# Banks, product buffers and the order of sums in a message-passing layer on one core

## The chip, the core and the metric

The kernel runs on one core of one Trainium2 chip, as one launch. The time is the device time in microseconds (us) of an execution. The kernel before was timed in three runs. A profile was taken of a further execution.

## What is computed

One layer of a graph network over 6,250 nodes of 128 features and 100,000 edges, which are sorted by their destination `dst`, all in float32:

```
msg_in = concatenate([x[src], x[dst], edge_attr], axis=1)      # 128 + 128 + 4
h = silu(msg_in @ mW1 + mb1)
messages = h @ mW2 + mb2
aggregated = segment_sum(messages, dst, N)
u = silu(concatenate([x, aggregated], axis=1) @ uW1 + ub1)
updated = u @ uW2 + ub2
out = layernorm(x + layer_norm(x + updated, ln_g, ln_b))
```

## The kernel before, in words

Edges are handled in 98 groups of 1,024 (G = 8 tiles of 128; the last group has 6 tiles). The first product is split: `x @ mW1[:128]` and `x @ mW1[128:256] + mb1` are computed once per node and kept as two tables in HBM, `tab_a` and `tab_b` (the table phase, L333 to L362). For an edge, `pre` is a row of `tab_a` (by its source), a row of `tab_b` (by its destination) and the four edge attributes times their weights. Since edges are sorted, the destinations of a group lie within a window of W = 96 nodes. So no second gather is needed: 96 rows of `tab_b` and the 4 rows of weights are loaded as the matrix `mv`, and a matrix `st` holds, for each edge, a one at its destination and its attributes. TensorE multiplies the two.

For each group g these steps are made; the names are those of the code.

- `fetch` (L272): eight gathers on GpSimd's queue (POOL), each of 128 rows of `tab_a` into the tile `ga`. `ga` has six buffers (AHEAD + 2), and gathers are issued four groups ahead. Groups 0 to 3 (RAW = 4) gather rows of x itself, since the table isn't there yet; gathers from group 4 on wait for `tab_a` to be written.
- `load` (L532): SP loads `mv` and the attribute rows of `st`, four groups ahead.
- `node_matrix` (L541): VectorE makes `st` (L543), three groups ahead.
- `products` (L564): TensorE's matmuls of `st` and `mv` into `pre` (L568). `pre` is a PSUM tile of two banks with three buffers, and products are made two groups ahead of their use.
- `hidden` (L577): VectorE adds `ga` and `pre` to `s` (L590), ScalarE applies silu and writes `h` (L591). For groups 0 to 3 TensorE transposes the rows (L583) into another `pre` buffer, VectorE copies them (L585), TensorE multiplies them by the weights (L572, between the matmuls of L568), and ScalarE applies silu (L586).
- `edge_matrix` (L553): VectorE makes `oh` (L556), the edges' one-hot matrix of the window, by comparing the node row `w_row` (0 to 95) with each edge's place `rel`; one group ahead.
- `by_nodes` (L594): TensorE transposes the counts of edges (L597) and sums h by node with `oh` (L600).
- `add` (L603): VectorE adds the sums to `acc` and the counts to `deg` (L606), at the window's place.

A node batch (`node_batch`, L410) computes the rest of the layer for four tiles of nodes as soon as their sums are complete, a stage per group (`advance`), with its products in the PSUM tile `y` of one bank; the last batch follows the last group.

The order on SP, TensorE, VectorE and ScalarE is the order of the code (`manual_schedule`, L107). In the step of group g of the loop at L613, that is: fetch g+4, load g+4, products g+2, hidden g, node_matrix g+3, edge_matrix g+1, by_nodes g-1, add g-2, and a stage of each running node batch. So the sums of a group stand behind the products of three groups later, and one step behind their h. On GpSimd's queue, the order within a group's gathers is left to the scheduler.

[...] `pre` takes six, `y` one, and `held_ps` (L169) one: it holds the sums of even groups, the sums of odd groups, and the node row `w_row` (L170).

Further, `hold` (L260) adds waits for TensorE to gathers. In the table phase one gather each of groups 2 and 3 waits for matmuls of that phase (L358); in the loop, one gather of each group from 9 on waits for the products of four groups before (L287).

Of the kernel before, what the change touches and what calls it, by code (L numbers as in the profile page):

```python
# [24 lines left out]
def kernel(  # L25
# [81 lines left out]
    edges.enter_context(tc.manual_schedule(engines={ENG.SP, ENG.PE, ENG.DVE, ENG.Activation}))  # L107
    gath = edges.enter_context(tc.tile_pool(name="gath", bufs=AHEAD + 2))
    work = edges.enter_context(tc.tile_pool(name="edge", bufs=2))
    ps = edges.enter_context(tc.tile_pool(name="edge_ps", bufs=2, space=PSUM))  # L110

    def wide():
        return ps.tile([P, G, P], F32, name="pre", bufs=3)

    def narrow():
        return wide()[:, :2, :].rearrange("p i f -> p (i f)")

    tables = ExitStack()
    tpool = tables.enter_context(tc.tile_pool(name="tables", bufs=1, side="right"))


    def by_group(a, pad):
# [43 lines left out]
    make_identity(nc, ident)  # L166
    w_row_i = consts.tile([P, W], I32, name="w_row_i")
    nc.gpsimd.iota(w_row_i, pattern=[[1, W]], base=0, channel_multiplier=0)
    held_ps = fixed.tile([P, 5 * W], F32, name="held_ps")  # L169
    w_row = held_ps[:, 4 * W :]  # L170
    nc.vector.tensor_copy(w_row, w_row_i)
    p_col_i = consts.tile([P, 1], I32, name="p_col_i")
    nc.gpsimd.iota(p_col_i, pattern=[[0, 1]], base=0, channel_multiplier=1)
# [81 lines left out]
    tab_b = dram.tile([NW, H], F32, name="tab_b")  # L255
    ea_d = dram.tile([ED, NG * GE], F32, name="ea_d")
    near_d = dram.tile([NG, GE], U8, name="near_d")
    rows, bases, near, opening, made = {}, {}, {}, {}, {}

    def hold(g, ins):  # L260

        tc.add_manual_dep(
            opening[g],
            ins.ins.name,
            mybir.DependencyInfo(mybir.DependencyClass.Sync, mybir.DependencyReason.DATA),
            reason="TensorE keeps up with the gathers",
        )

    def tiles_of(g):
        return min(G, -(-(E - g * GE) // P))  # L270
# [1 line left out]
    def fetch(g):  # L272
        if g >= NG:
            return
        rows[g] = gath.tile([P, G, H], F32, name="ga")
        for i in range(tiles_of(g)):
            ins = nc.gpsimd.indirect_dma_start(  # L277
                out=rows[g][:, i, :],
                out_offset=None,
                in_=x if g < RAW else tab_a[:, :],  # L280
                in_offset=bass.IndirectOffsetOnAxis(
                    ap=src_i[:, g, i : i + 1] if g else src_0[:, i : i + 1], axis=0
                ),
            )
            if i == 0:
                opening[g] = ins.ins
                if g - AHEAD in made:  # L287
                    hold(g, made[g - AHEAD])

    for g in range(RAW):  # L290
        fetch(g)
# [47 lines left out]
    for k, (i0, n) in enumerate(parts):  # L339
        if k + 1 < len(parts):  # L340
            turn_x(*parts[k + 1])

        tb = x_sb[:, i0 : i0 + n, :]
        ta = tpool.tile([P, G, H], F32, name="t", bufs=2)
        for j0, m in groups(n, G // 2):
            pm = wide().rearrange("p (i s) f -> p i s f", s=2)
            for j in range(m):
                cols = slice((i0 + j0 + j) * P, (i0 + j0 + j + 1) * P)
                ins = nc.tensor.matmul(pm[:, j], xT[:, cols], w1, start=True, stop=True)  # L349
            own = slice(j0, j0 + m)  # L350
            nc.scalar.copy(ta[:, own], pm[:, :m, 0, :])
            nc.vector.tensor_add(  # L352
                tb[:, own], pm[:, :m, 1, :], b1[:, None, :].to_broadcast([P, m, H])
            )
        nc.sync.dma_start(by_node(tab_b)[:, i0 : i0 + n, :], tb)
        nc.sync.dma_start(by_node(tab_a)[:, i0 : i0 + n, :], ta[:, :n])
        if k in (1, 3):
            hold(k // 2 + 2, ins)  # L358
        cols = slice(i0 * P, NW if i0 + n == NT else (i0 + n) * P)
        nc.vector.memset(acc[:, cols], 0.0)  # L360
        nc.vector.memset(deg[:, cols], 0.0)
# [6 lines left out]
    if E < NG * GE:  # L368
        pad = tpool.tile([ED, NG * GE - E], F32, name="pad")
        nc.vector.memset(pad, 0.0)  # L370
        nc.sync.dma_start(ea_d[:, E:], pad)
    tables.close()


    w2u = consts.tile([P, H], F32, name="w2u")
# [20 lines left out]
            nc.sync.dma_start(t, row.rearrange("(o f) -> o f", o=1).to_broadcast([P, H]))  # L396

    def fuse_weights():
        pt = narrow()
        nc.tensor.transpose(pt[:, :P], raw_w["w2"], ident)  # L400
        w2T = work.tile([P, P], F32, name="w2T", bufs=1)
        nc.scalar.copy(w2T, pt[:, :P])
        pm = narrow()
        nc.tensor.matmul(pm[:, :H], w2T, raw_w["u1a"], start=True, stop=True)
        nc.tensor.matmul(pm[0:1, H:], raw_w["mb2"], raw_w["u1a"], start=True, stop=True)
        nc.scalar.copy(w2u, pm[:, :H])
        nc.scalar.copy(mb2u, pm[0:1, H:])


    def node_batch(i0, n, work, new, y):  # L410
# [83 lines left out]
        yield  # L494
        nc.sync.dma_start(rows_of(out), o[:m, :n])

    def node_tiles(pool, ps):
        return (
            pool,
            lambda name, p=P: pool.tile([p, BT, H], F32, name=name),  # L500
            lambda: ps.tile([P, BT, H], F32, name="y"),
        )

    def advance(running):

# [9 lines left out]
        hbuf.append(held.tile([P, G, H], F32, name=f"h{k}"))  # L515
    NST = 5
    nodes = edges.enter_context(tc.tile_pool(name="nodes", bufs=1))
    node_ps = edges.enter_context(tc.tile_pool(name="node_ps", bufs=1, space=PSUM))
    stbuf = [held.tile([K1, GE], F32, name=f"st{k}") for k in range(NST)]

    def load_bases(g):
# [40 lines left out]
        return oh  # L562

    def products(g, xg=None):  # L564
        pre = wide()
        st = stbuf[g % NST].rearrange("k (i c) -> k i c", i=G)
        for i in range(tiles_of(g)):
            ins = nc.tensor.matmul(  # L568
                pre[:, i, :], st[:, i, :], mv[g % NM], start=True, stop=xg is None
            )  # L570
            if xg is not None:
                nc.tensor.matmul(pre[:, i, :], xg[:, i, :], w1[:, 0, :], start=False, stop=True)  # L572
        if xg is None:
            made[g] = ins
        return pre

    def hidden(g):  # L577
        h = hbuf[g % NH]
        ga = rows.pop(g)
        if g < RAW:  # L580
            px = wide()
            for i in range(G):
                nc.tensor.transpose(px[:, i, :], ga[:, i, :], ident)  # L583
            xg = work.tile([P, G, P], F32, name="s")
            nc.vector.tensor_copy(xg, px)  # L585
            nc.scalar.activation(h, products(g, xg), AF.Silu)  # L586
        else:
            n = tiles_of(g)
            s = work.tile([P, G, H], F32, name="s")
            nc.vector.tensor_add(s[:, :n], ga[:, :n], pre.pop(g)[:, :n])  # L590
            nc.scalar.activation(h[:, :n], s[:, :n], AF.Silu)  # L591
        return h

    def by_nodes(g, h, oh):  # L594

        pt = held_ps[:, g % 2 * 2 * W : (g % 2 + 1) * 2 * W]
        nc.tensor.transpose(pt[0:1, W:], deg_g[:, g : g + 1], ident[:W, :W])  # L597
        n = tiles_of(g)
        for i in range(n):
            nc.tensor.matmul(pt[:, :W], h[:, i, :], oh[:, i, :], start=i == 0, stop=i == n - 1)  # L600
        return pt
# [11 lines left out]
    for g in range(NG + 1):  # L613
        if g == 3:
            load_weights()
        if g == 5:
            fuse_weights()
        for c in range(1, NC):
            if g == max(1, c * EC // GE - 10):
                attributes(c)  # L620
            if g == max(1, c * EC // GE - 10) + 1:
                attribute_rows(c)
        if g + AHEAD >= RAW:
            fetch(g + AHEAD)
        if g + LEAD < NG:
            load(g + LEAD)
        if g >= RAW:
            for k in range(g if g == RAW else g + MADE - 1, min(g + MADE, NG)):
                pre[k] = products(k)
        if g < NG - 1:  # L630
            h[g] = hidden(g)
        if g + MADE < NG:
            node_matrix(g + MADE)
        if g + 1 < NG:
            oh[g + 1] = edge_matrix(g + 1)
        if 0 <= g - 1 < NG:
            pt[g - 1] = by_nodes(g - 1, h.pop(g - 1), oh.pop(g - 1))
        for k in range(max(g - 2, 0), g - 1 if g < NG - 1 else g):
            if k in pt:
                add(k, pt.pop(k))  # L640
        for i0, n, first in batches:
            if g == min(first + 1, NG):
                tiles = node_tiles(nodes, node_ps)
                if first == NG:

                    tiles = (
                        nodes,
                        lambda name, p=P: gath.tile([P, G, H], F32, name="ga")[:p, :BT],
                        lambda: wide()[:, :BT],
                    )  # L650
                running.append(node_batch(i0, n, *tiles))
        advance(running)
        if g >= NG - 2:
            advance(running)
        if g == NG - 1:
            h[g] = hidden(g)
    while running:
        advance(running)
    edges.close()
# [1 line left out]
    def all_nodes():  # L661
        with tc.tile_pool(name="nodes_g", bufs=2) as nodes:
            with tc.tile_pool(name="nodes_g_ps", bufs=1, space=PSUM) as node_ps:
                for i0, n, _ in batches:
                    running = [node_batch(i0, n, *node_tiles(nodes, node_ps))]
                    while running:
                        advance(running)

# [145 lines left out]
```

## Time and profile before

| | |
|---|---|
| three timed runs | 1029.84, 1030.1 and 1032.72 us; median 1030.1 us |
| profiled execution | 1330.47 us, span 1328.6 us |
| mean granted clock of TensorE | 0.678 |
| POOL (gathers) | busy 738.9 us in 790 instructions, 782 of them gathers of 943 ns |
| TensorE's matmuls | busy 685.9 us |
| VectorE | busy 485.2 us |
| ScalarE | busy 238.9 us |
| DMA | 88.95 MB, 67 GB/s over the span |

The profiled execution is one execution, and longer than the timed runs by 300 us. "Span" is from the program's first instruction to its last. In rows of the timeline the first number is the start, the second the time taken, both in us; then engine, line, operation and the tiles written and read; in brackets stands the engine's idle time ahead of the row and what ended it. In rows of the waits: who waited, for whom, the sum in us, how many times, and the longest. "issue" means that the profile shows nothing that was waited for, "remote" a semaphore whose last update it can't put to an instruction.

### The profile page before, as it was taken

Reading aid. Unit: us, or ns where it says so; the run is one execution under the profiler, and the core shown is the slowest. Engines: PE = TensorE matmul, PEld = TensorE weight load, DVE = VectorE, ACT = ScalarE, POOL = GpSimd, SP = SyncE. Lnnn points to the kernel's source line nnn. Section 1 sums busy time; section 2 is a strip of 40 time slices with the busy share of each in tenths; the row PEclk is TensorE's granted clock in tenths of the full one; section 3 lists DMA queues with packets and bytes.
Section 4 is the critical chain, followed back from the end, with each engine's and each line's share of the span. In section 5 each row is a group of like instructions: output and inputs, shape, how many; then the busy total and the mean of one; then the engine's idle time right before and its main releaser. Section 6 shows DMA issues by size and latency. Waiting matters only on the chain.

```text
span 1328.6 us, 11337 instructions
## 1 busy us (share of the span) xinstructions
PE 685.9 (52%) x3696; PEld 605.2 (46%) x3696; DVE 485.2 (37%) x1018; ACT 238.9 (18%) x294; POOL 738.9 (56%) x790
## 2 busy tenths in 40 slices
PE   3737756434733553455563364445544555543665
PEld 3526645433633453355453354345433445443553
DVE  1643333243334333334233334233334334334443
ACT  1301111012112111112121112111202202202223
POOL 6266666645654655566655655555655666645500
PEclk9867777666766675676666767666866766766765
DMA  6733222112312212222212211222212222212100
GB/s 171 214 94 82 70 62 78 50 36 54 93 44 67 72 47 63 54 69 70 76 45 64 70 51 49 76 54 68 79 44 60 60 67 74 73 42 54 50 7 24
DMA packets 69916, 88.95 MB, mean 67 GB/s; under 512 B 20671, under 2 KB 51534, under 8 KB 69850
## 3 DMA queue, kind: packets, MB, share of 16 engines
q0 software_dynamic: 25024, 51.30, 15.3%
q1 hardware_dynamic: 41290, 35.08, 9.2%
q10 hardware_dynamic: 3536, 1.77, 0.5%
q8 instruction: 31, 0.51, 0.2%
q14 instruction: 35, 0.29, 0.1%
HBM read 76.71 MB, written 11.38 MB: 66 GB/s over the span
## 4 chain that ended last, share of the span: by engine, by line
another core or an unknown queue 34%; issue 23%; DVE 21%; PE 11%; POOL 6%; DMA 3%; DVEq 1%; ACT 1%; SPq 0%; ACTq 0%; POOLq 0%
DVE st L543 7%; PE held_ps L600 6%; POOL ga L277 6%; DVE oh L556 5%; DVE s L590 2%; PE pre L568 2%; DVE z L476 1%; DVE y L473 1%; DMA ga<-tab_a,src_i 1%; DVE st L427 1%; DVE mv L428 1%; DVEq L590 1%; PE y L446 1%; DMA mv<-tab_b 1%
## 5 line engine op out<-in xcount | busy, mean ns | idle before, releaser
L277 POOL DMA_INDIRECT ga<-tab_a,src_i x750 | 707.5, 943 | 495.5 <-issue 371.7
L597 PE MATMUL held_ps<-ident,deg_g 96*1 96x96 f32 x98 | 28.6, 292 | 533.5 <-DVE oh L556 474.1
L606 DVE TENSOR_TENSOR acc<-acc,held_ps 128x96 f32 x98 | 24.9, 254 | 730.7 <-remote 497.6
L600 PE MATMUL held_ps<-oh,h 128*128 128x96 f32 x1564 | 287.7, 362 | 0.3 <-ACT h L591 0.3
L600 PEld LDWEIGHTS held_ps<-oh,h 128*128 128x128 f32 x1564 | 276.9, 274 | 1.6 <-ACT h L591 0.7
L568 PE MATMUL pre<-mv,st 100*128 100x128 f32 x1564 | 260.6, 327 | 31.4 <-issue 31.4
L568 PEld LDWEIGHTS pre<-mv,st 100*128 100x128 f32 x1564 | 245.7, 242 | 41.5 <-issue 40.0
L597 PEld LDWEIGHTS held_ps<-ident,deg_g 96*1 96x1 f32 x98 | 8.2, 83 | 551.5 <-DVE oh L556 487.2
L591 ACT ACTIVATE h<-s 128x1024 f32<-128x1024 f32 x94 | 99.1, 1054 | 713.3 <-DVE s L590 576.8
L543 DVE TENSOR_SCALAR_CACHE_REDUCE st<-near,p_next 96x1024 f32<-96x1024 uint8 x98 | 124.2, 1269 | 1.6 <-DMA ea_d<-pad 1.6
L590 DVE TENSOR_TENSOR s<-ga,pre 128x1024 f32<-128x1024 f32 x94 | 114.4, 1217 | 28.1 <-DMA ga<-tab_a,src_i 10.7
L556 DVE TENSOR_TENSOR oh<-held_ps,rel 128x768 f32<-128x768 f32 x98 | 93.0, 949 | 0.0
L591 ACT ACT_TABLE_LOAD x21 | 26.9, 1283 | 124.3 <-DVE s L590 83.2
L349 PE MATMUL pre<-w,xT 128*128 128x256 f32 x98 | 25.9, 420 | 12.9 <-DVE x_sb L352 11.7
L277 POOL DMA_INDIRECT ga<-in_x_dram,src_i x24 | 22.6, 943 | 15.6 <-PE pre L349 6.9
L433 ACT ACT_TABLE_LOAD x24 | 30.8, 1283 | 2.7 <-DVE mv L428 2.3
L462 PEld LDWEIGHTS y<-u,uT 128*128 128x128 f32 x94 | 22.7, 327 | 17.6 <-issue 17.6
L572 PE MATMUL pre<-w,s 128*128 128x128 f32 x64 | 18.4, 383 | 21.0 <-DVE s L585 15.9
L349 PEld LDWEIGHTS pre<-w,xT 128*128 128x128 f32 x98 | 20.0, 211 | 17.3 <-DVE x_sb L352 13.2
L462 PE MATMUL y<-u,uT 128*128 128x128 f32 x94 | 26.2, 460 | 0.0
L441 ACT COPY acc_b<-acc 128x512 f32<-128x512 f32 (+1 forms) x12 | 7.3, 609 | 102.0 <-DVE acc L606 66.4
L572 PEld LDWEIGHTS pre<-w,s 128*128 128x128 f32 x64 | 15.0, 289 | 21.8 <-DVE s L585 16.3
(117 smaller groups left out, 399.4 us busy)
## 6 DMA issues: line engine op xcount, KB each, us to landing
ga<-tab_a,src_i POOLq DMA_INDIRECT x750
near<-near_d SPq DMA_DIRECT2D x24, 384.0 KB
mv<-tab_b SPq DMA_DIRECT2D x98, 48.0 KB
tab_b<-x_sb SPq DMA_DIRECT2D x6, 512.0 KB
tab_a<-t SPq DMA_DIRECT2D x6, 512.0 KB
xs<-in_x_dram SPq DMA_DIRECT2D x11, 256.0 KB
out_dram<-z SPq DMA_DIRECT2D x11, 256.0 KB
st<-ea_d SPq DMA_DIRECT2D x98, 16.0 KB
```

The lines of the kernel that those rows point to most:

```text
L277: ins = nc.gpsimd.indirect_dma_start(out=rows[g][:, i, :], out_offset=None, in_=x if g < RAW else tab_a[:, :], in_offset=bass.IndirectOffs ...
L349: ins = nc.tensor.matmul(pm[:, j], xT[:, cols], w1, start=True, stop=True)
L433: nc.scalar.activation(r[:, :n], mv[:, :n, 1], AF.Sqrt, bias=eps)
L462: nc.tensor.matmul(y[:, i, :], by_p[:, :, i], u2, start=False, stop=i == n - 1)
L543: nc.vector.tensor_scalar(stbuf[g % NST][:W], near.pop(g), p_next, 0.0, op0=OP.is_equal, op1=OP.add, accum_out=deg_g[:, g : g + 1],)
L556: nc.vector.tensor_tensor(oh, w_row[:, None, :].to_broadcast([P, G, W]), rel[:, g, :, None].to_broadcast([P, G, W]), op=OP.is_equal,)
L568: ins = nc.tensor.matmul(pre[:, i, :], st[:, i, :], mv[g % NM], start=True, stop=xg is None)
L572: nc.tensor.matmul(pre[:, i, :], xg[:, i, :], w1[:, 0, :], start=False, stop=True)
L590: nc.vector.tensor_add(s[:, :n], ga[:, :n], pre.pop(g)[:, :n])
L591: nc.scalar.activation(h[:, :n], s[:, :n], AF.Silu)
L597: nc.tensor.transpose(pt[0:1, W:], deg_g[:, g : g + 1], ident[:W, :W])
L600: nc.tensor.matmul(pt[:, :W], h[:, i, :], oh[:, i, :], start=i == 0, stop=i == n - 1)
```

## The change

- The node row `w_row` becomes a tile of its own, in a bank of its own.
- The sums go to `pt`, a tile of one bank with two buffers, so that even and odd groups have a bank each.
- `pre` has two buffers instead of three. The table phase has its own pool with three buffers of two banks, which is closed before the loop's PSUM tiles are made.
- In the step of group g, products of g+2 come after hidden g (the add of `ga` and `pre`, which frees a buffer), and the sums of g come right behind that in the same step, where before those of g-1 stood. The adds of g-2 stay, and stand ahead of the sums.
- The holds of gathers are taken out.
- `fuse_weights`, once, at group 5, uses the tile of the node batches instead of a `pre` buffer.

```diff
-    ps = edges.enter_context(tc.tile_pool(name="edge_ps", bufs=2, space=PSUM))
+    tables_ps = tables.enter_context(tc.tile_pool(name="tables_ps", bufs=3, space=PSUM))
     def wide():
-        return ps.tile([P, G, P], F32, name="pre", bufs=3)
+        return tables_ps.tile([P, G, P], F32, name="wide")
...
-    held_ps = fixed.tile([P, 5 * W], F32, name="held_ps")
-    w_row = held_ps[:, 4 * W :]
+    w_row = fixed.tile([P, W], F32, name="w_row")
...
-            if i == 0:
-                opening[g] = ins.ins
-                if g - AHEAD in made:
-                    hold(g, made[g - AHEAD])
...
-        if k in (1, 3):
-            hold(k // 2 + 2, ins)
...
     tables.close()
+    ps = edges.enter_context(tc.tile_pool(name="edge_ps", bufs=2, space=PSUM))
+    node_ps = edges.enter_context(tc.tile_pool(name="node_ps", bufs=1, space=PSUM))
+    def rows_ps():
+        return ps.tile([P, G, P], F32, name="pre")
+    def node_y():
+        return node_ps.tile([P, BT, H], F32, name="y")
...
     def by_nodes(g, h, oh):
-        pt = held_ps[:, g % 2 * 2 * W : (g % 2 + 1) * 2 * W]
+        pt = ps.tile([P, 2 * W], F32, name="pt")
...
-        if g >= RAW:
-            for k in range(g if g == RAW else g + MADE - 1, min(g + MADE, NG)):
+        if g == RAW:
+            for k in (g, g + 1):
                 pre[k] = products(k)
-        if g < NG - 1:
+        last = g >= NG - 1
+        if not last:
             h[g] = hidden(g)
+        if g >= RAW and g + 2 < NG:
+            pre[g + 2] = products(g + 2)
         if g + MADE < NG:
             node_matrix(g + MADE)
         if g + 1 < NG:
             oh[g + 1] = edge_matrix(g + 1)
-        if 0 <= g - 1 < NG:
-            pt[g - 1] = by_nodes(g - 1, h.pop(g - 1), oh.pop(g - 1))
-        for k in range(max(g - 2, 0), g - 1 if g < NG - 1 else g):
+        for k in range(g - 2, g - 1 if not last else g):
             if k in pt:
                 add(k, pt.pop(k))
+        if not last:
+            pt[g] = by_nodes(g, h.pop(g), oh.pop(g))
...
         if g == NG - 1:
-            h[g] = hidden(g)
+            pt[g] = by_nodes(g, hidden(g), oh.pop(g))
```

## The prediction

> **What bounds the kernel now.** I read the first part of the page for the engines' shares, the waits, and then the timeline, first of the gather queue alone and then of all engines.
>
> ```profile
> PE 685.9 (52%) x3696; PEld 605.2 (46%) x3696; DVE 485.2 (37%) x1018; ACT 238.9 (18%) x294; POOL 738.9 (56%) x790
> ```
> ```profile
> DVE acc L606 <- remote: 497.6, 42, 17.4
> PE held_ps L597 <- DVE oh L556: 474.1, 54, 18.1
> POOL ga L277 <- issue: 380.6, 734, 10.3
> ```
>
> No engine is full. The second and third lines are two halves of one loop. TensorE's sums (L597, L600) wait for the edge matrix (L556), and VectorE's adds (L606) wait for the sums: the node row, which L556 reads, and both halves of the sums lie in one bank, `held_ps`. But 1330.5 us is the profiled execution's time, against a median of 1030.1 us, so I ask which waits the timed runs can hold.
>
> ```profile
> 599.37 0.94 POOL L277 DMA_INDIRECT ga<-tab_a,src_i  x1 [0.30 <-issue]
> 600.62 0.94 POOL L277 DMA_INDIRECT ga<-tab_a,src_i  x1 [0.30 <-issue]
> ...
> 609.71 0.94 POOL L277 DMA_INDIRECT ga<-tab_a,src_i  x1 [3.16 <-issue]
> ```
>
> Gathers follow each other every 1.248 us (0.94 and 0.30) unless the queue is stopped, here by 3.16 us at a group's first gather, whose buffer comes free when L590 of six groups earlier has ended (608.97). 782 gathers take 975.9 us. The first starts at 4.0 and the last ends at 1255.2, so stops make up 1255.2 - 4.0 - 975.6 = 275.6 us. After it comes the last group's L590 at 1302.9, 25.7 us before the end of the span.
>
> The same account for the timed runs: 1030.1, less 1.9 outside the span, less 25.7 of tail, less 1.1 for the last gather's landing, less 4.0 and 975.6, leaves 21.8 us of stops in all. If a gather costs the same there, **some 254 us of the profile's stops are absent from the timed runs, and the gather queue is their bound**, 9.98 us a group.
>
> ```profile
> 618.85 1.95 PE L600 MATMUL held_ps<-oh,h 128*128 128x96 f32 x16
> 626.78 0.25 DVE L606 TENSOR_TENSOR acc<-acc,held_ps 128x96 f32 x1 [8.07 <-remote]
> ```
>
> This is what is absent: recorded matmuls end at 620.80, and the add that needs them starts at 626.78. By durations alone the loop needs 1.22 (L590) + 1.27 (L543) + 0.95 (L556) + 3.83 (until the add) + 0.49 (two adds), less overlaps, 7.7 us from 607.75 to 615.42. That is under 9.98.
>
> **What the Trainium skill says.** "PSUM — Partial Sum Buffer", PSUM bank collisions: two engines may not touch one bank and quadrant together, whatever the address, so software guards by bank. The trace agrees: L597 waits for L556, whose data it doesn't use. "Perfetto Trace Analysis", Tensor Engine Instruction: a matmul's end is estimated, not observed. The trace agrees (the 6 us above); so I trust matmul starts and durations as capacity, and not as completions. "TensorE: Matmul & The Clock Gate", What's actually happening: the array's clock halves after an idle window. The trace has both: 16 matmuls of L600 take 1.95 or 3.62 us, and the mean granted clock is 0.678. "DMA: Bandwidth & Descriptors", Anatomy of one DMA: some 2.0 us fixed for one such DMA; less the 0.94 of issue that gives my landing of 1.1, an estimate.
>
> **The change part by part.**
>
> *Own banks for the node row and for even and odd sums.* Removes the loop above. In the timed runs its 7.7 us lie beneath 9.98 of gathers, so I cost it at nothing; if the queue did wait for it, the bound is the 21.8 us. The added tiles issue no new instruction.
>
> *Two product buffers instead of three.* Products of g+2 now wait for L590 of g. They take 1.98 to 3.67 us (128-column rows of L568) and are wanted two groups, 20 us, later: nothing. Queued behind them are the sums of g and the node batches; all are met within the 9.98.
>
> *Sums of g right behind h of g.* In the main groups TensorE stands idle for ScalarE's 1.06 us (L591) in a period with at least 9.98 - 7.3 = 2.7 us to spare (7.3 is 3.67 and 3.62 on the slow clock): nothing. In **groups 0 to 3**, where rows of x are transposed and multiplied, it counts.
>
> ```profile
> 81.39 1.21 DVE L585 COPY s<-pre 128x1024 f32<-128x1024 f32 x1
> ...
> 88.41 1.04 PE L583 MATMUL pre<-ident,ga 128*128 128x128 f32 x8
> ...
> 101.69 0.94 POOL L277 DMA_INDIRECT ga<-tab_a,src_i  x1 [4.80 <-remote]
> 102.51 1.02 ACT L586 ACTIVATE h<-pre 128x1024 f32<-128x1024 f32 x1
> ...
> 108.77 1.95 PE L600 MATMUL held_ps<-oh,h 128*128 128x96 f32 x16
> ```
>
> Before, TensorE goes from a group's products to the sums of the group before, whose h is long done, and to the next transposes. After, it waits for this group's L586, and the next group's transposes (L583) queue behind that. Each of four groups adds 1.02 and two hand-overs of 0.12: 1.26 x 4 = 5.0. The activation table's load ahead of the first L586 (1.28) moves onto this path once. And sums of group 3 now stand ahead of products of group 4: 2.05 (with the degree's transpose), 3.7 on the slow clock. So L590 of group 4 comes 8.3 us later, or 10.0.
>
> Who waits for it: gathers of group 10 reuse the rows of group 4. Unhindered, their first is due 48 gathers after group 4's first: 67.25 + 59.9 = 127.2. Before, with recorded durations and no late completions: products of group 0 end at 88.6; three rounds of transposes 1.04, copy 1.35, products 6.1 and sums 2.0 end at 120.0; products of group 4 and 5 at 122.0 and 124.0. One gather of group 9 waits for the latter by the hold and takes 1.25: **125.2, 2.0 us early**. After: 120.0 + 8.3 + 2.0 + 1.32 (hand-over, L590) = 131.6, **4.4 us late**. On the slow clock (products 6.8, transposes 1.91, sums 3.7, 3.67 for plain products) before is 12.3 us late and after 18.7: 6.4 us more. A table phase that ends earlier moves both sides alike.
>
> *Gathers without holds.* One of each group's eight waited for TensorE. The table phase's holds (6.92 and 1.95 us of stops at 39.65 and 51.27) stand ahead of 15.04 us in which the queue waits for the table anyway: 0, the stop only moves. From group 9 on: the credit is already taken above (products of group 5 plus a gather). Later products are done three groups before their gather: 0.
>
> *The rest.* Separate table buffers, three as before; fusing weights in the y bank takes a wait off for product buffers: 0, at most -1. Node batches keep their place. SP issues the same DMAs in the same order.
>
> Sum: 4.4 to 6.4. Against that, VectorE of before needs up to 11.5 us from L590 of group 4 to that of 5, and afterwards 7.7, so it could stop the queue again for 0 to 3 us while it catches up; after doesn't. I take +5. In the profile's own frame that is 1330.5 + 5, but its late completions make that sum worthless there; for the timed runs, 1030.1 + 5 = **1035 us**.
>
> **Rivals.** *No change:* the timed runs keep over 6 us of slack at group 10, as the table may hold the queue longer there than VectorE's lists; 1030. For it: the quick chain has slack already. Against: 21.8 us of stops leave little room for the table's 23.3 (67.25 - 4.0 - 32 x 1.248) to be longer. *Faster:* the table phase stops the queue only for some 10 us in the timed runs (ScalarE's 11.4 us wait at 34.23 is a late completion), and the other 12 are stops at main-loop openings, where VectorE and TensorE wait for each other through `held_ps`. Own banks and free gathers remove these, less 4 lost at the start: 1022. It decides once node batches lift the loop over 9.98 for six groups together. Against: a batch's rows (L464 to L485) sum to some 8 us of VectorE for 7.5 groups, and 7.7 + 1.1 is still below 9.98. *Slower still:* the hold's gather wasn't late, so no credit, and the clock is slow: all 10.0 us, 1040. *The change not done:* no; in the built order sums follow products of g+2 directly, and each later group's gathers keep only a wait for VectorE.
>
> **How the numbers follow.** About 0.3% (3.1 us) is what this measurement tells from no change. Forecast, 1033.3 to 1038: 0.48. Slower still: 0.12. No change: 0.27. Faster: 0.13. So slower 0.60, same 0.27, faster 0.13. The range 1026 to 1041 leaves out most of the faster case and the end of the slowest, under 0.2.
>
> **What would show it.** In the profile after: adds (L591) with almost no wait; sums no longer waiting for the edge matrix; in groups 0 to 3, sums waiting for L571, and first gathers of groups 7 to 10 stopped longer. Gathers stay at 1.248 us, and no stop comes from TensorE behind group 9. I am wrong if timed runs fall below 1027: then the loop, not the queue, set the time.

## The result, and the profile after

The changed kernel takes 1023.03 us (median of five runs, 1021.98 to 1025.49), the kernel before 1030.1 us in the same comparison. The ratio is 0.993, with a 95% interval of 0.9912 to 0.9948: 0.7% faster, where I had forecast 0.5% slower. These times, and all in the next part, are of chips on which the kernel before takes 1026 to 1033 us; on two other chips it takes 1277 to 1340 us, as in the profile shown ahead of the prediction, and the runs made there have a part of their own below. A ratio compares, for each kernel, its runs within 1.5% of its fastest, so on those two chips, where the runs of one kernel spread by more, it isn't the ratio of the medians.

The lines that answer to those shown of before, from the page, the waits and the timeline of the changed kernel (span 1021.3 us). Its line numbers differ: L268 is the gather (L277 before), L568 the transposes (L583), L571 their silu (L586), L575 the addition into s (L590), L543 the edge matrix (L556), L582 and L585 the sums (L597 and L600), L591 the add to `acc` (L606).

```profile
PE 685.0 (67%) x3696; PEld 618.4 (61%) x3696; DVE 477.2 (47%) x1018; ACT 238.2 (23%) x294; POOL 741.8 (73%) x790
```
```profile
DVE s L575 <- DMA ga<-tab_a,src_i: 450.5, 85, 9.3
POOL ga L268 <- issue: 226.1, 742, 0.3
...
DVE acc L591 <- PE pt L585: 4.9, 1, 4.9
```
```profile
599.27 0.94 POOL L268 DMA_INDIRECT ga<-tab_a,src_i  x1 [0.30 <-issue]
...
600.93 1.95 PE L585 MATMUL pt<-oh,h 128*128 128x96 f32 x16
605.65 1.22 DVE L575 TENSOR_TENSOR s<-ga,pre 128x1024 f32<-128x1024 f32 x1 [6.06 <-DMA ga<-tab_a,src_i]
...
608.86 0.24 DVE L591 TENSOR_TENSOR acc<-acc,pt 128x96 f32 x1
```

The engines are as busy as before. VectorE's addition (L575) now waits for gathers, 85 times and 450 us in all, and the adds (L591) find their sums ready. The queue has 742 waits of at most 0.3 us each, the step from one gather to the next: it is the bound.

Which of this is the gain? For that I needed a profile of the kernel before on a chip where it takes 1030 us (the run b_plain, below). The account of the two spans, read from the queue's timeline and from VectorE's last addition into s:

| part of the span, us | before (b_plain) | after |
|---|---|---|
| start to first gather | 4.1 | 4.1 |
| 782 gathers, stops taken out | 977.6 | 978.9 |
| stops of the queue | 7.9 | 9.3 |
| end of the last gather to end of the last addition into s | 14.0 | 3.6 |
| from there to the end | 24.7 | 25.3 |
| span | 1028.3 | 1021.3 |

The queue stops no less after the change than before. **The whole gain, 10.4 us less 3.4 us given back in the other parts, lies behind the last gather.** A further profile of either order agrees: from there to the start of the last addition it is 13.1 us in b_plain and 13.0 in b_notabhold, 2.7 after the change and 2.5 in a_loophold. Here is the end of the kernel before, in the timeline of b_plain; its last gather is issued until 989.53:

```profile
975.90 3.62 PE L600 MATMUL held_ps<-oh,h 128*128 128x96 f32 x16
...
985.93 0.32 PE L597 MATMUL held_ps<-ident,deg_g 96*1 96x96 f32 x1 [6.41 <-DVE oh L556]
...
986.05 3.62 PE L600 MATMUL held_ps<-oh,h 128*128 128x96 f32 x16
...
989.71 0.26 DVE L606 TENSOR_TENSOR acc<-acc,held_ps 128x96 f32 x1 [3.83 <-PE held_ps L600]
...
993.23 1.65 PE L446 MATMUL y<-xT,u1x 128*128 128x384 f32 x2 [3.56 <-DVE z L476]
...
997.77 3.62 PE L600 MATMUL held_ps<-oh,h 128*128 128x96 f32 x16
...
1001.50 0.25 DVE L606 TENSOR_TENSOR acc<-acc,held_ps 128x96 f32 x1 [6.73 <-PE held_ps L600]
...
1002.63 0.95 DVE L590 TENSOR_TENSOR s<-ga,pre 128x768 f32<-128x768 f32 x1
```

And the end of the changed kernel, whose last gather is issued until 992.31:

```profile
989.25 3.62 PE L585 MATMUL pt<-oh,h 128*128 128x96 f32 x16
...
993.76 0.25 DVE L591 TENSOR_TENSOR acc<-acc,pt 128x96 f32 x1
...
994.99 0.95 DVE L575 TENSOR_TENSOR s<-ga,pre 128x768 f32<-128x768 f32 x1 [0.18 <-DMA ga<-tab_a,src_i]
```

Before, VectorE waits twice for sums, and the last group's addition stands behind both waits. The add at 989.71 is that of group 94, whose own sums (975.90) had ended at 979.52. It waits 3.83 us for the sums of group 95 (986.05), which write the other half of its bank; and these, whose h had long been there, had waited for the edge matrix of group 97, which reads the node row in the same bank. It is so all the way: in b_plain the adds of groups 0 to 95 start 0.04 to 0.11 us behind the end of the sums of the group after theirs, and at least 6.0 us behind the end of their own. (Row and sums are also one tile of the program; no run separates the tile from the bank.) Then 6.73 us, before the adds of groups 95 and 96: the sums of group 96 stand one step later in TensorE's queue, behind a node batch's products (L446 to L448), which wait for VectorE themselves. After the change the sums of 96 run at 989.25, ahead of the batch, and VectorE waits for neither. The two waits make 10.6 us, the account 10.4.

### The profile page after: what moved, and what is told of

Same layout as the page of the kernel before. It is cut to its first block, busy times and chain, and to the rows that moved or that the text cites. A ratio compares the mean times of both kernels' runs of the same rounds, so it can differ in the third digit from the quotient of the medians.

```text
span 1021.3 us, 11233 instructions
## 1 busy us (share of the span) xinstructions
PE 685.0 (67%) x3696; PEld 618.4 (61%) x3696; DVE 477.2 (47%) x1018; ACT 238.2 (23%) x294; POOL 741.8 (73%) x790
## 4 chain that ended last, share of the span: by engine, by line
POOL 53%; issue 24%; DMA 7%; DVE 6%; PE 4%; ACT 1%; DVEq 0%; POOLq 0%; ACTq 0%
POOL ga L268 53%; DMA ga<-tab_a,src_i 7%; PE pt L585 1%; PE pre L555 1%; DVE st L530 1%; DVE z L468 1%; DVE oh L543 1%; DVE y L465 1%; PE pre L559 1%; DVE st L419 1%; DVE mv L420 1%; PE pre L568 0%; DVE s L570 0%; ACT h L571 0%; DVE s L575 0%
## 5 line engine op out<-in xcount | busy, mean ns | idle before, releaser
L268 POOL DMA_INDIRECT ga<-tab_a,src_i x750 | 710.5, 947 | 237.9 <-issue 216.7
L555 PE MATMUL pre<-mv,st 100*128 100x128 f32 x1564 | 319.0, 382 | 277.3 <-DVE s L575 223.9
L555 PEld LDWEIGHTS pre<-mv,st 100*128 100x128 f32 x1564 | 293.2, 286 | 299.0 <-DVE s L575 243.0
L575 DVE TENSOR_TENSOR s<-ga,pre 128x1024 f32<-128x1024 f32 x94 | 114.4, 1217 | 469.7 <-DMA ga<-tab_a,src_i 450.5
L585 PE MATMUL pt<-oh,h 128*128 128x96 f32 x1564 | 247.9, 326 | 5.5 <-ACT h L571 5.5
L585 PEld LDWEIGHTS pt<-oh,h 128*128 128x128 f32 x1564 | 243.5, 245 | 12.4 <-ACT h L571 6.6
L543 DVE TENSOR_TENSOR oh<-w_row,rel 128x768 f32<-128x768 f32 x98 | 92.9, 948 | 0.0
L582 PE MATMUL pt<-ident,deg_g 96*1 96x96 f32 x98 | 32.0, 327 | 9.1 <-DVE deg L591 8.9
L454 PEld LDWEIGHTS y<-u,uT 128*128 128x128 f32 x94 | 22.7, 327 | 10.4 <-issue 10.4
L268 POOL DMA_INDIRECT ga<-in_x_dram,src_i x24 | 22.6, 944 | 7.3 <-issue 7.3
L591 DVE TENSOR_TENSOR acc<-acc,pt 128x96 f32 x98 | 23.6, 241 | 4.9 <-PE pt L585 4.9
L336 PE MATMUL wide<-w,xT 128*128 128x256 f32 x98 | 24.1, 403 | 0.0
L591 DVE TENSOR_TENSOR deg<-deg,pt 1x96 f32 x98 | 23.1, 235 | 0.0
L336 PEld LDWEIGHTS wide<-w,xT 128*128 128x128 f32 x98 | 19.5, 205 | 2.9
```

What stands on the lines that cost most here:

```text
L268: nc.gpsimd.indirect_dma_start(out=rows[g][:, i, :], out_offset=None, in_=x if g < RAW else tab_a[:, :], in_offset=bass.IndirectOffsetOnAx ...
L454: nc.tensor.matmul(y[:, i, :], by_p[:, :, i], u2, start=False, stop=i == n - 1)
L543: nc.vector.tensor_tensor(oh, w_row[:, None, :].to_broadcast([P, G, W]), rel[:, g, :, None].to_broadcast([P, G, W]), op=OP.is_equal,)
L555: nc.tensor.matmul(pre[:, i, :], st[:, i, :], mv[g % NM], start=True, stop=xg is None)
L591: nc.vector.tensor_add(at, at, of)
```

## Experiments on chips where the kernel before takes 1030 us

**The kernel before again, and without the table phase's holds.** First the unchanged kernel (b_plain), for its profile:

> The kernel before, unchanged, on a chip where it takes about 1030 us: what its profile lacked. By my account of the timed runs its gather queue stops for some 22 us in all. Theory table phase (holds or shared buffers): all of the surplus over the changed kernel's 7 to 9 us lies ahead of the first gather of group 4. Theory order or bank: it lies in stops at groups 6 to 15. If neither, it lies after the last gather, in the tail.

1030.14 us; the account stands above. The stops are 7.9 us, not the 22 of my account. The cause is neither the table phase's holds nor the openings of the loop; it is the third case, the tail. The queue has one stop, in the timeline of the queue:

```profile
43.11 0.94 POOL L277 DMA_INDIRECT ga<-in_x_dram,src_i  x1 [0.30 <-PE pre L349]
52.26 0.94 POOL L277 DMA_INDIRECT ga<-tab_a,src_i  x1 [8.21 <-DMA mv<-in_L_gnn_mW_dram]
```

This is the first gather of group 4, which waits for the table. The hold ahead of it costs nothing (0.30).

```diff
-        if k in (1, 3):
-            hold(k // 2 + 2, ins)
```

> The kernel before without the table phase's two holds (gathers of groups 2 and 3 no longer wait for the table's matmuls); the loop's holds stay. My prediction said that these holds cost nothing, as their stops only replace the wait for the table: then 1030. If they push the first table gather later, up to 8.9 us less (6.92 and 1.95, the two stops in the first profile): 1021 to 1026.

1029.63 us against 1029.53, ratio 0.9997 (0.9987 to 1.0008): the table phase's holds cost nothing, as predicted.

**The loop's holds put back into the changed kernel** (`hold` and its call in `fetch`, with the products' last matmul in `made`):

```diff
...
+            if i == 0:
+                opening[g] = ins.ins
+                if g - AHEAD in made:
+                    hold(g, made[g - AHEAD])
...
```

> The changed kernel with the loop's holds alone put back (a gather of each group from 9 on waits for products of four groups earlier); the table phase's gathers stay free. Where the kernel before takes about 1300 us: if the loop's holds bring the 100 us that separate the changed kernel with both kinds of hold (1208) from it without (1313), again about 1208; if the table phase's holds bring them by shifting the start, 1313. Where before takes 1030: theory holds 1029 to 1031, every other theory 1022 to 1024.

1022.62 us, ratio to before 0.9925 (0.9901 to 0.9949), with one stop of the queue (7.3 us, the table): the loop's holds cost nothing either.

**Even and odd sums in one bank again, the node row apart:**

```diff
+    held_ps = fixed.tile([P, 4 * W], F32, name="held_ps")
...
-        pt = ps.tile([P, 2 * W], F32, name="pt")
+        pt = held_ps[:, g % 2 * 2 * W : (g % 2 + 1) * 2 * W]
```

> The changed kernel with even and odd sums in one bank again, the node row in a bank of its own. Where before takes about 1300 us: if it is the row's place in the sums' bank that costs (the kernel before gained 5% when the row alone left it), no slower than the changed kernel, 1313; if the two halves' sharing costs as well, between that and 1352, the time with all three in one bank. Where before takes 1030: theory bank 1026 to 1031, theories holds and order 1022 to 1024.

1023.85 us, ratio 0.994 (0.9918 to 0.9962); the last addition starts 2.9 us behind the last gather's issue, 2.7 in the changed kernel. In the new order of sums, that the halves have a bank each brings nothing that these times show.

**Sums of all groups one group later, as before, all else changed:**

```diff
+        if 0 <= g - 1 < NG:
+            pt[g - 1] = by_nodes(g - 1, h.pop(g - 1), oh.pop(g - 1))
         for k in range(max(g - 2, 0), g - 1 if not last else g):
...
-        if not last:
-            pt[g] = by_nodes(g, h.pop(g), oh.pop(g))
...
         if g == NG - 1:
-            pt[g] = by_nodes(g, hidden(g), oh.pop(g))
+            h[g] = hidden(g)
```

> The changed kernel with the sums of a group one group later, as before the change, all else kept; this time where the kernel before takes about 1030. If the order of the sums is the gain, 1028 to 1031. If it cost 4 us at the start as I predicted, or nothing as the two profiles with a stop only at the table suggest, 1021 to 1024.

1027.49 us, ratio 0.998 (0.9972 to 0.9988), between the two kernels. Its timeline behind the last gather (issued until 990.64) has one of the two waits left:

```profile
981.29 1.95 PE L585 MATMUL pt<-oh,h 128*128 128x96 f32 x16
...
995.41 3.62 PE L585 MATMUL pt<-oh,h 128*128 128x96 f32 x16
...
999.07 0.26 DVE L591 TENSOR_TENSOR acc<-acc,pt 128x96 f32 x1 [6.24 <-PE pt L585]
...
999.87 0.95 DVE L575 TENSOR_TENSOR s<-ga,pre 128x768 f32<-128x768 f32 x1
```

The sums of group 95 (981.29) now run as soon as those of 94 are done, before the edge matrix of 97 (986.48); those of 96 still follow the node batch. The last addition starts 9.2 us behind the last gather, 13.1 before and 2.7 after. So the order is worth 6.5 us of that stretch, and the rest of the change 3.9. The wait that is gone went through both shared places, from the edge matrix to the sums by the row and from the sums to the add by the other half, so I put the 3.9 down to own banks. That is read from two timelines. The row's move alone is enough to take this wait away, by a trace from a chip where TensorE is slow (b_rowsbuf, below); the halves' bank alone in the old order, and the changed order of products with two buffers, were not tried by themselves.

**The order of the last groups alone.** In the kernel before, group 96 in the new order (b_endsums), and in the changed kernel, group 96 in the old one (a_endlate):

```diff
-        if 0 <= g - 1 < NG:
+        if g - 1 in h:
             pt[g - 1] = by_nodes(g - 1, h.pop(g - 1), oh.pop(g - 1))
...
                 add(k, pt.pop(k))
+        if g == NG - 2:
+            pt[g] = by_nodes(g, h.pop(g), oh.pop(g))
```

> The kernel before with the sums of the last group but one (96) issued right behind its hidden layer, ahead of that step's node batch, as the change does; the order of all other groups, the shared bank, the holds and the three product buffers stay. Theory end: this alone brings most of the change's 7 us: the last group's addition starts some 3 us after the last gather's issue instead of 13.1, and the time is 1021 to 1025. Rival, that the steady order of all groups does it: 1029 to 1030.

```diff
+        if g == NG - 1:
+            pt[g - 1] = by_nodes(g - 1, h.pop(g - 1), oh.pop(g - 1))
         for k in range(g - 2, g - 1 if not last else g):
...
-        if not last:
+        if g < NG - 2:
             pt[g] = by_nodes(g, h.pop(g), oh.pop(g))
```

> The changed kernel with the sums of group 96 alone issued one step later, behind the node batch, as before the change; all other groups keep the new order. Theory end: as with all sums late, 1026 to 1029, and the last group's addition starts about 9 us after the last gather's issue. Rival, steady order: 1022 to 1024.

b_endsums takes 1025.35 us, ratio 0.9964 (0.9952 to 0.9977): a little above what I wrote down, but 4.0 of the 7 us (1029.32 on that chip, less 1025.35) come from where one group of 98 stands in a queue. a_endlate takes 1026.95, ratio 0.9978 (0.9969 to 0.9986): by the same edit the other way it is 3.9 us above the changed kernel's 1023.03, or 4.9 by the two ratios, as these two were timed apart. Its last addition starts 8.9 us behind the last gather, 9.2 in a_late2, and the times are the same: with own banks, the order of the other 97 groups brings nothing that these times show. In the timeline of b_endsums, whose last gather is issued until 988.78, the second wait is gone:

```profile
989.69 3.62 PE L600 MATMUL held_ps<-oh,h 128*128 128x96 f32 x16
...
994.19 0.26 DVE L606 TENSOR_TENSOR acc<-acc,held_ps 128x96 f32 x1
...
995.32 0.95 DVE L590 TENSOR_TENSOR s<-ga,pre 128x768 f32<-128x768 f32 x1
```

The last addition starts 6.5 us behind the gather, not 13.1, but not the 3 I expected either: the rest down to 2.7 is the first wait, which this edit leaves. Of the 6.6 us gained, 1.2 are given back behind the addition (25.9 us to the end instead of 24.7), where the node batch is now later. This profile took 1023.98 us, the least of nine runs, so 1.4 of the rest are not in it.

**Five raw groups, to make the queue reach the start's charge.** The changed kernel with RAW = 5 instead of 4 (a_raw5), and the same with the sums of the raw groups alone one group later (a_best):

```diff
+        if 0 < g <= RAW:
+            pt[g - 1] = by_nodes(g - 1, h.pop(g - 1), oh.pop(g - 1))
         for k in range(g - 2, g - 1 if not last else g):
...
-        if not last:
+        if RAW <= g < NG - 1:
             pt[g] = by_nodes(g, h.pop(g), oh.pop(g))
```

> The changed kernel with five groups of raw rows ahead of the table instead of four: the queue has 12.5 us, less the time of issue, to fill while the table is made, so its stop of 7 to 8 us at the first table gather goes. The stage of raw groups gets one longer by about 11 us more on TensorE and VectorE. If nothing else stopped the queue, 1015 to 1016. With early sums in the raw groups my predicted charge at the start now shows: the first additions of table groups come 50 us after their gathers already with four, so gathers of groups 10 and 11 stop for some 5 to 10 us, and the time is 1018 to 1023.

> Five raw groups, and the sums of the raw groups one group later as before the change; from the first table group on the changed order. With the early sums' charge taken off the raw groups (the first table group's addition came 15 us earlier in the kernel before than in the changed one), the queue should not stop at groups 10 and 11, so 1014 to 1017, below both kernels. If the raw stage is still too long by a few us, 1017 to 1020.

a_raw5 takes 1021.79 us: its stop for the table is gone, and another has come in its place, in the queue's timeline:

```profile
73.27 0.94 POOL L268 DMA_INDIRECT ga<-tab_a,src_i  x1 [0.30 <-issue]
80.44 0.94 POOL L268 DMA_INDIRECT ga<-tab_a,src_i  x1 [6.22 <-PE pre L568]
```

It stands at group 7, not at 10 or 11 as I expected: group 7 reuses the buffer of raw group 1, whose transposes queue behind the sums of group 0. In a_best they don't, and the queue never stops, in its waits:

```profile
POOL ga L268 <- issue: 228.6, 750, 0.3
```

a_best takes 1015.38 us (1015.06 to 1015.69), ratio to the kernel before 0.9869 (0.9848 to 0.989), faster than both kernels. So the early sums of raw groups do cost 6.4 us (1021.79 less 1015.38) once the queue has no stop for the table in which to hide them.

## The runs where TensorE is slow

The experiments above were made on chips 5, 6 and 14. Seven other runs, and two meant for the part above, were made on chips 4 and 7, where the kernel before takes 1277 to 1340 us; each is compared with the kernel before on the same chip.

> The kernel before, unchanged. Asked: is the profiled execution again far above the timed runs, with TensorE's completions arriving in blocks? If those late completions belong to this kernel's structure (waits of the gather queue on TensorE, or the shared bank), the profile is again above 1200 us. If the first profile was a chance event of one execution, it is within 5 us of 1030, and its stops sum to about 22 us; then this profile shows where the 7 us lie.

> The changed kernel as it is, on the chip of this call, to set the scale. Where the kernel before takes about 1030 us on this chip, 1022 to 1024. Where it takes about 1315, TensorE's matmuls complete late there: if holds alone make the loss in that case, about 1200 or above (as the changed kernel with holds, 1208); if gathers that wait for TensorE cost on top, well below, 1030 to 1150.

The kernel before took 1318.11 us in its own run against 1315.22: neither of the two cases that I wrote down, as here the timed runs are as long as the profile. The changed kernel took 1313.28 against 1300.38, ratio 1.0116 (1.0027 to 1.0205): no gain there. Nor do the holds make the loss, as I had thought possible: with them the changed kernel takes 1208 us (a_holds, below). What is different is TensorE, and it shows in two forms. In the changed kernel's timeline in a_same:

```profile
628.18 1.95 PE L585 MATMUL pt<-oh,h 128*128 128x96 f32 x16
...
644.07 0.52 PE L585 MATMUL pt<-oh,h 128*128 128x96 f32 x1 [1.09 <-issue]
646.15 0.32 PE L585 MATMUL pt<-oh,h 128*128 128x96 f32 x1 [1.57 <-issue]
647.57 0.52 PE L585 MATMUL pt<-oh,h 128*128 128x96 f32 x1 [1.10 <-issue]
...
656.65 1.82 PE L585 MATMUL pt<-oh,h 128*128 128x96 f32 x8 [0.38 <-issue]
```

Sixteen matmuls take 1.95 us at 628. From 630 on they come in short bursts, and from 638 to 656 one at a time, 0.7 to 2.1 us from start to start, with nothing in the profile that they wait for. From one matmul to the next of the same line, more than 0.8 us pass 286 times in this profile, 525 us in all; in the same kernel's profile at 1023 us 3 times, 5.8 us in all.

In the kernel before, on the same chip (b_same), that is rare: 45 times, 61 us. There the ends are late: 44 adds start 1.2 to 14.8 us behind the recorded end of the sums that they wait for, 332 us in all, and in b_plain none. This is the form that the profile ahead of the prediction has.

The queue stops for some 254 us in a_same, so it isn't the bound there. The granted clock tells little of it: 0.672 against 0.734 in the mean, and 0.50 from 640 to 656, where at the half clock 16 matmuls otherwise take 3.62 us.

The other kernels there, with their edits where not shown above: b_noholds is the kernel before without both kinds of hold, a_holds the changed kernel with both, a_late the kernel of a_late2; a_onebank and b_rowsbuf are

```diff
-    w_row = fixed.tile([P, W], F32, name="w_row")
+    held_ps = fixed.tile([P, 5 * W], F32, name="held_ps")
+    w_row = held_ps[:, 4 * W :]
...
-        pt = ps.tile([P, 2 * W], F32, name="pt")
+        pt = held_ps[:, g % 2 * 2 * W : (g % 2 + 1) * 2 * W]
```
```diff
-    w_row = held_ps[:, 4 * W :]
+    w_row = consts.tile([P, W], F32, name="w_row")
```

> The kernel before without its holds (no gather waits for a matmul of the table phase or of the products); all else as before. Theory holds: the 7 us are gathers that waited for TensorE, so 1022 to 1025, and the profile comes down with it. Theory bank: the node row and both halves of the sums in one bank stop the loop, so 1029 to 1031. Theory table phase: the separate table buffers or the order of the sums did it, 1029 to 1031 as well.

> The changed kernel with the holds put back, in the table phase and on the products. Theory holds: 1029 to 1031. Theory bank and theory table phase: 1022 to 1024, as the changed kernel.

> The changed kernel with the node row and both halves of the sums back in one bank, no holds. Theory bank: 1028 to 1031, with adds that wait for sums and sums that wait for the edge matrix. Theory holds and theory table phase: 1022 to 1024, since the loop of 7.7 us stays under the 9.98 us of a group's gathers.

> The kernel before with one line changed: the node row lies in SBUF, so that the edge matrix touches no PSUM bank; both halves of the sums stay in one bank. Theory bank by the node row (sums wait for the edge matrix and it for them): most of the change's gain, so 1022 to 1026 where before takes 1030, and near the changed kernel where before takes 1315. Theory bank by even and odd sums, theory order: as before within 0.3% where before takes 1030.

> The changed kernel with the sums of a group one group later, as before the change, all else kept. My prediction charged the early sums with 8.3 us at the start of groups 0 to 3 and 4 us of them at group 10. If that charge is right this is faster than the changed kernel, by at most the 2 us that its queue still stops at groups 8 and 10 where it takes 1023: 1021 to 1023. If the order of the sums is where the gain comes from, it is slower: 1028 to 1031.

| run | us | kernel before, us | ratio to it (95%) |
|---|---|---|---|
| b_noholds | 1331.96 | 1315.22 | 1.0355 (1.0286 to 1.0425) |
| a_holds | 1207.85 | 1315.22 | 0.9398 (0.9336 to 0.946) |
| a_onebank | 1352.22 | 1315.22 | 1.0504 (1.0431 to 1.0576) |
| b_rowsbuf | 1236.73 | 1300.38 | 0.954 (0.9468 to 0.9613) |
| a_late | 1319.33 | 1300.38 | 1.0184 (1.0117 to 1.0251) |

Most of these expectations were written for 1022 to 1031 us, and none of the times speaks on the 7 us. The one guess for the slow case in them missed: b_rowsbuf is far below the changed kernel, not near it. In their own frame the parts of the change pull in opposite ways: with the node row in the sums' bank the changed kernel is slower than before (its six runs all lie above the eleven of before), with the row alone moved the kernel before gains 5%, and the waits of gathers for TensorE, free of cost elsewhere, take 8% off the changed kernel here (1207.85 against 1313.28). By the medians b_noholds is 1.3% slower than the kernel before. Why waits for TensorE help, and what makes it slow, no run here shows.

The end of b_rowsbuf's timeline does bear on the first of the two waits, which is 3.83 us in b_same as in b_plain:

```profile
1199.64 1.95 PE L600 MATMUL held_ps<-oh,h 128*128 128x96 f32 x16
1201.63 0.26 DVE L606 TENSOR_TENSOR acc<-acc,held_ps 128x96 f32 x1
```

The sums of group 95 no longer stand behind the edge matrix of 97 (1200.57), and the add of group 94 has hardly a wait (0.12 us), with the halves still in one bank and the order as before.

Last, the two runs meant for the questions above, on chip 7. In b_end3 the kernel before has groups 95 and 96 in the new order (the condition of b_endsums is `g in (NG - 3, NG - 2)`); a_rawlate is a_best with four raw groups.

> The kernel before with the sums of groups 95 and 96, its last but two and last but one, right behind their hidden layers; all other groups, the shared bank, the holds and the three product buffers as before. Theory end: the last addition starts 2.5 to 3.5 us behind the last gather's issue and the time is 1021 to 1024, the whole of the change's gain. Rival, that own banks or the steady order bring the remaining 2 to 3 us: 1025, as with group 96 alone.

> The changed kernel, four raw groups, with the sums of the raw groups alone one group later as before the change. What my prediction charged to the start as 4.4 to 6.4 us is at most the stops that the changed kernel's profiles show at groups 8 and 10, 1.3 us in one and none in two: so 1021 to 1023, the same as the changed kernel. If the charge were real, 1017 to 1019.

They took 1318.32 us, ratio 0.9956 (0.9896 to 1.0017), and 1325.5 us, 1.0188 (1.0104 to 1.0273), which answers neither by the time. But the end of b_end3's timeline shows what this order does with the shared bank kept:

```profile
1276.76 3.62 PE L600 MATMUL held_ps<-oh,h 128*128 128x96 f32 x16
...
1280.41 0.96 DVE L556 TENSOR_TENSOR oh<-held_ps,rel 128x768 f32<-128x768 f32 x1 [2.45 <-PE held_ps L600]
1281.29 0.24 DVE L606 TENSOR_TENSOR acc<-acc,held_ps 128x96 f32 x1
...
1286.37 0.25 DVE L606 TENSOR_TENSOR acc<-acc,held_ps 128x96 f32 x1
```

Neither the add of group 94 (1281.29) nor that of 95 (1286.37) waits. The edge matrix of 97 waits 2.45 us for the sums of 95 instead, as the additions of groups 95 and 96 are 6.5 us apart there; in b_plain they are 10.1 apart, which leaves these sums more room. So the order of two groups takes both waits away without any own bank, and whether it makes the whole gain where the kernel takes 1030 us stays open. So does what the early sums of four raw groups cost by a run rather than by the stops in a profile.

## Why the prediction was wrong

I had the kernel 5 us slower, and it is 7 us faster. The charge at the start came to 1.3 us or none, and what the change does behind the last gather, 10.4 us, was put at nothing.

**The gather queue as the bound: right.** 1.249 us from gather to gather in the median, 1.248 predicted. My sign of being wrong misled: I wrote that under 1027 us "the loop, not the queue, set the time", and at 1023 the queue still sets it until the last gather.

**The account of the timed runs: wrong, and the step that failed first.** I took off "1.1 for the last gather's landing" and what was left, 21.8 us, was "stops in all". In b_plain the stops are 7.9 us, and from the last gather's end to the last addition it is 13.1 us to its start and 14.0 to its end. The 21.8 are thus 7.9 of stops, 12.0 more behind the last gather than I took off, and 2.0 by which the gathers take longer (977.6, not 975.6). The landing isn't my estimate of 1.1 us either, with which issue and landing make 2.0: in the changed kernel, additions that wait for gathers start 1.7 us behind the end of the last one's issue in the median. The profile of before had shown the place: I had the last gather's end at 1255.2 and the last L590 at 1302.9, and left the 47.7 us between them out of the account for the timed runs, without asking what stood ahead of L590 in VectorE's queue.

**Own banks, "at nothing": right for 96 groups, wrong for the end.** The loop of 7.7 us does lie beneath the 9.98 us of gathers (L606 waited for sums 97 times in b_plain, 327 us, and all but the last few at no cost: L590 still waited 158 us for gathers). After the last gather nothing covers it: 3.9 us, with the sums in their old order. In the full change the early sums of group 95 would take the same wait away, by b_end3's trace, so what the banks add there isn't shown. "If the queue did wait for it" was the only way to a cost that I asked for. I also misread the wait: "the add that needs them" at 626.78 is of the group before and doesn't need those sums; they share its bank. And the 6 us that I put to a matmul's estimated end belong to the slow TensorE: in b_plain adds follow the recorded ends by 0.04 to 0.11 us.

**Sums right behind h, "nothing" in the main groups: the same.** I wrote that what is queued behind is met within the 9.98 us and that "node batches keep their place". They did, but the sums of group 96 passed ahead of one, and that is 6.5 us of the last stretch (some 4 of the total by either flip).

**Groups 0 to 3, +4.4 to 6.4: right in mechanism, wrong in slack.** The sums wait for L571 and the transposes behind them, in the timeline after:

```profile
75.60 3.73 PE L585 MATMUL pt<-oh,h 128*128 128x96 f32 x16 [2.36 <-ACT h L571]
...
79.12 1.91 PE L568 MATMUL pre<-ident,ga 128*128 128x128 f32 x8
```

L590 of group 4 was to come 8.3 us later; from 97.17 (b_plain) to 105.04 (a_loophold, table 0.7 us earlier) it is 7.9, and 14.8 in the changed kernel's profile, where this stage has 13.7 us at half clock. But I gave the kernel before 2.0 us of slack at group 10, and it has 13.8: due 52.26 + 59.9 = 112.2, addition done at 98.4 (by the hold's gather, which my 2.0 were for, it is 12.0). Most of that is the term of a raw group, 10.5 us, three times: it took 7.7, as its products take 3.6 us at full clock and not 6.1. So stops of 1.3 us (groups 8 and 10 of the changed kernel's profile) or none (a_loophold, a_halves), instead of 4.4. With five raw groups the charge is there, 6.4 us, but at group 7 and by the transposes. On the slow clock, my figures give 11.3 and 17.7 us late, not 12.3 and 18.7; the difference of 6.4 stays.

**Holds: right,** 1029.63 and 1022.62 us. The halves' own banks bring nothing in the new order either, 1023.85 us. Two product buffers instead of three were not tried alone.

**The rivals.** "Faster" named 1022 us, and 1023 came, but its mechanism was wrong as well: it had 12 us of stops at the loop's openings, and b_plain has none. That its number came is luck.

"PSUM — Partial Sum Buffer", PSUM bank collisions, bore on more than I drew from it. Guarding by bank and not by address, as it tells software to do, accounts for two waits here: the one that I cited, of sums for an edge matrix whose data they don't use (the 6.41 us of idle TensorE at 985.93), and that of an add for sums which it doesn't use (the 3.83 us of VectorE at 989.71). Both are on the path there.

## What to carry to other kernels

A loop that hides beneath a bound hides only while the bound runs: after the last transfer, everything that is queued ahead of the last piece of work on each engine is paid in full. Cost a change of order three times, for the start, for a middle step, and for the last two steps by writing out each engine's queue there. And when an account of a span leaves a remainder, find its place in a timeline before naming it.

## What the runs showed of the hardware

The same kernel took 1026 to 1033 us on chips 5, 6 and 14 and 1277 to 1340 us on chips 4 and 7, with TensorE late in the profiles of the latter. In the changed kernel (a_same) single matmuls start 0.7 to 2.1 us apart, for up to some 30 us at a time, where 16 take 1.95 us otherwise; in the kernel before (b_same) 44 adds start 1.2 to 14.8 us behind the recorded end of the sums they wait for. The mean granted clock hardly shows it (0.672 against 0.734). Where a profile and the timed runs of one kernel differ by 300 us, the profile may be of another chip, and its waits are then not those of the timed runs.
